# A three-layer interaction network on one core: four chunks' h1 kept, M in array quarters, V1 and V0 moved to VectorE

## The chip, the cores and the metric

The kernel runs on one core of a Trainium2 chip. The metric is the device time of one execution in microseconds, taken as the median of three timed runs. A profile of one more execution shows, for every engine, what ran when and what ended each wait.

## What is computed

The input x has 1024 samples, 64 fields and 16 embedding columns (all float32). Three layers multiply the field matrix with itself:

```python
x0 = x; h = x; xs = []
for i in range(3):
    z = einsum('bfe,bge->bfge', x0, h).reshape(B, 64 * fh, 16)
    y = einsum('oc,bce->boe', W[i], z) + b[i]
    if i != 2:
        x_i, h = y[:, :64], y[:, 64:]
    else:
        x_i, h = y, y
    xs.append(x_i)
out = sum(concatenate(xs, axis=1), axis=2) @ fc_w.T + fc_b
```

## The kernel before, in words

Everything behind the hidden halves is linear up to the final sum, so the kernel never forms layers two and three in full. With u = x1 (the hidden half of layer one, "h1") the result is a sum over products of two factors. The kernel makes h1 = W0[64:]·z, a second factor from a 64x64x64 array M (W1[64:] contracted with V2, where V2 is W2 weighted by fc_w) and V1 (W1[:64] weighted by fc_w), and a term in V0 (W0[:64] weighted by fc_w).

The 1024 samples are cut into 32 chunks of 512 columns. For each chunk c, `product(c, j)` on VectorE makes four z tiles of 128x2048 (line 159), and `contract` / `contract_last` (lines 167 and 183) multiply 16 slices of z and one last tile `zl` with `w_all`, 17 weight tiles of 128 columns: columns 0 to 63 give h1 ("part 0"), columns 64 to 127 give the second factor ("part 1"). A whole chunk is 17 matmuls, and each float32 matmul appears as two records. `factors` then multiplies the two halves, `sums` reduces them, `v0x` adds the V0 term once for each pair of chunks.

Part 1 of `w_all` is not there at the start. The setup is a chain: W2 is loaded and weighted (line 273, `pv2`), copied and written back transposed (`v2t`), M is made by 64x64 matmuls (line 296, `pm`) and copied to `m_sb` (line 297), `m_sb` is written to DRAM as `md` (lines 298 to 304), read back skewed as `ms` on the SP and ACT queues (lines 330 and 335), and added into part 1 of `w_all` (line 341). While this goes on, the first NF = 3 chunks go through `side_by_side` (line 224): 64 weight columns, two column halves of the chunk beside each other in the array, part 0 only. When part 1 is there, the same three chunks are run with part 1. Their z tiles are kept until then; the pool `zp` has 13 of them. V1 and V0 are made by eight matmuls on TensorE (line 355, `pv01`), copied by ScalarE and moved into `w_all` and `bd` by DMA.

The order of the instructions on each engine and on each queue is the order of the program text. The tile pools decide when a buffer can be written again: `xa` and `xb` have two buffers each, the `set` tiles of the setup two.

Of the kernel before, what the change touches and what calls it, by code (L numbers as in the profile page):

```python
# [45 lines left out]
NF = 3  # L46
# [3 lines left out]
def cin_kernel(ctx, tc, xra, xrb, w0p, w0d, w1h, wv2, w01, b0, b1, b2, fc_w, fc_b, out):  # L50
# [52 lines left out]
    fv2 = const_tile("fv2", [128, 32])  # L103
    fv01 = const_tile("fv01", [128, 32])
    nc.gpsimd.memset(fv01, 0.0)
    nc.gpsimd.tensor_copy(fv2, fc2.to_broadcast([128, 32]))
    for n in range(2):
        nc.gpsimd.tensor_copy(
            fv01[halves[n], 16 * n : 16 * n + 16], fc01[halves[n]].to_broadcast([F, 16])
        )  # L110
# [60 lines left out]
    def last_tile(c):  # L171

        zl = xp.tile([128, N], F32, tag="zl", name=f"zl_{c}", bufs=4)
        nc.scalar.activation(zl[0:64], xas[c][0:64, 0, :], AF.Square)  # L174
        nc.scalar.copy(zl[64:128], xas[c][64:128, 0, :])  # L175
        if c % 2 == 0:
            xxs[c // 2] = sp.tile([128, N], F32, tag="xx", name=f"xx_{c}", bufs=3)
        to = halves[c % 2]
        nc.scalar.copy(xxs[c // 2][to], xas[c][to, 0, :])  # L179
        zls[c] = zl  # L180
# [25 lines left out]
    def sums(k, rows, parts):  # L206
# [7 lines left out]

    H2 = N // 2

    def side_by_side(c, part, tiles):
        cols = slice(part * F, (part + 1) * F)  # L220
        for t in tiles:
            z = zls[c] if t == NT else zs[c, t // NI][:, t % NI, :]
            for n in range(2):
                nc.tensor.matmul(  # L224
                    accs[c][halves[n], part * H2 : (part + 1) * H2],
                    w_all[:, t, cols], z[:, n * H2 : (n + 1) * H2],
                    start=(t == 0), stop=(t == NT), skip_group_check=True,
                )

    def group(j):  # L230
        return range(j * NI, (j + 1) * NI)

    def first_factors(c):
        uu = uu_tile(c)
        q = sp.tile([128, H2], F32, tag="q", name=f"q_{c}")
        nc.scalar.copy(q, accs[c][:, H2:N])
        for n in range(2):
            at = halves[n]
            nc.vector.scalar_tensor_tensor(
                uu[:, n * H2 : (n + 1) * H2], accs[c][at, 0:H2], bh1[at], q[at],  # L240
                ALU.add, ALU.mult,
            )

    def h1_weights(tiles):
# [4 lines left out]
    for c in range(NF):
        new_acc(c)  # L250
    last_tile(0)
    product(0, 0)
    h1_weights(slice(0, NI))
    side_by_side(0, 0, group(0))
    product(0, 1)

    nc.vector.memset(w0s[64:128, 3 * NI, 1, :], 0.0)
    h1_weights(slice(NI, NT))
    nc.vector.tensor_copy(w_all[0:64, NT, 0:64], w0ds)
    side_by_side(0, 0, group(1))  # L260
    product(0, 2)
    side_by_side(0, 0, group(2))
    product(0, 3)
# [20 lines left out]
    side_by_side(0, 0, group(3))  # L284
    side_by_side(0, 0, [NT])
# [4 lines left out]
    m_sb = z_tile("m_sb").rearrange("p i n -> p (i n)")  # L290
    m_lo, m_hi = [m_sb[to].rearrange("p (f g) -> p f g", g=F) for to in halves]
    for m in range(4):
        pm = ps.tile([128, 512], F32, tag="set", name=f"pm_{m}")
        cols = slice(m * 512, (m + 1) * 512)
        for to in halves:
            nc.tensor.matmul(pm[to], v2t[to], w1s[to, cols], start=True, stop=True)  # L296
        nc.scalar.copy(m_sb[:, cols], pm)
    nc.scalar.dma_start(out=md[0:64, 0:32, :], in_=m_lo)
    nc.scalar.dma_start(out=md[0:64, 32:64, :], in_=m_hi)
    nc.sync.dma_start(out=md[0:64, 64:96, :], in_=m_lo)  # L300
    nc.sync.dma_start(out=md[64:96, 32:64, :], in_=m_hi[0:32])
    nc.scalar.dma_start(out=md[64:96, 0:32, :], in_=m_lo[0:32])
    nc.sync.dma_start(out=md[64:96, 64:68, :], in_=m_lo[0:32, 0:4, :])  # L303
    nc.sync.dma_start(out=md[64:68, 68:96, :], in_=m_lo[0:4, 4:32, :])

    last_tile(1)
    for j in range(NJ):
        product(1, j)
        side_by_side(1, 0, group(j))
    side_by_side(1, 0, [NT])  # L310
    last_tile(2)
    for j in range(NJ):
        product(2, j)
        side_by_side(2, 0, group(j))
    side_by_side(2, 0, [NT])
# [35 lines left out]
    v01r = const_tile("v01r", [128, 2, 512])  # L351
    for n in range(2):
        pv = ps.tile([128, 512], F32, tag="set", name=f"pv01_{n}")
        for k in range(4):
            nc.tensor.matmul(  # L355
                pv[32 * k : 32 * k + 32], fv01, w01s[n][:, k * 512 : (k + 1) * 512],
                start=True, stop=True,
                tile_position=(0, 32 * k),
            )
        nc.scalar.copy(v01r[:, n, :], pv)  # L360
        v0, v1 = [
            v01r[16 * v : 128 : 32, n, :].rearrange("k (f g) -> k f g", g=F) for v in range(2)
        ]
        at = slice(32 * n, 32 * n + 32)
        nc.scalar.dma_start(out=w_all[64 + 32 * n : 96 + 32 * n, NT, 64:128], in_=v1)
        for to in halves:
            nc.scalar.dma_start(out=bd[to.start + 32 * n : to.start + 32 * n + 32, to], in_=v0)
    for c in range(3, 5):
        last_tile(c)
        for j in range(NJ):  # L370
            product(c, j)
# [126 lines left out]
```

## Time and profile before

| | us |
|---|---|
| median of three runs | 535.95 (535.71 to 536.26) |
| the profiled execution | 535.2 |
| its span in the trace | 533.4 |
| TensorE busy | 500.3 |
| VectorE busy | 341.4 |
| ScalarE busy | 81.7 |

Times in the rows count from the start of the span. A chain row gives start, length and what the chain of work went through. A timeline row gives start, length, engine, line, operation and how many instructions are merged in it. The profiled execution takes 1.8 us more than its span, and the median 0.75 us more than the profiled execution.

### The profile page before, as it was taken

The numbers are of one execution on the slowest core, as the hardware profiler recorded it, in microseconds if no ns is written. First come the engines' busy times: TensorE is split into PE (matmuls) and PEld (weight loads), VectorE is DVE, ScalarE is ACT, GpSimd is POOL, SyncE is SP. The second block draws the span as 40 slices with busy tenths as digits, with TensorE's granted clock in tenths as the row PEclk, the third lists the DMA queues.
The fourth block names the chain that finished last, engine by engine and source line by source line (L and its number), as shares of the span: only waits on it lengthen the run. The fifth ranks groups of instructions, "written<-read, shape, count | busy, mean of one in ns | idle before, by whom it ended". The sixth has DMA issues, their size and how long they took to land.

```text
span 533.4 us, 3675 instructions
## 1 busy us (share of the span) xinstructions
PE 500.3 (94%) x1490; PEld 228.2 (43%) x1490; DVE 341.4 (64%) x203; ACT 81.7 (15%) x141; POOL 7.0 (1%) x23
## 2 busy tenths in 40 slices
PE   2769299999999999999999999999999999999996
PEld 1336165444444444444444444444444444444442
DVE  3592159998939487694939487593939487591103
ACT  2012005111111111011111111011111111010001
POOL 5000000000000000000000000000000000000000
PEclk9979699999999999999999999999999999999999
DMA  7937774564443405144443505144443505100000
GB/s 266 422 114 179 192 334 159 204 237 194 159 157 127 188 20 227 69 157 159 157 157 120 194 17 222 77 159 157 158 157 114 202 11 227 79 0 0 0 1 0
DMA packets 14373, 76.97 MB, mean 144 GB/s; under 512 B 4336, under 2 KB 4880, under 8 KB 5396
## 3 DMA queue, kind: packets, MB, share of 16 engines
q1 hardware_dynamic: 12072, 74.81, 37.0%
q10 hardware_dynamic: 1964, 1.92, 1.7%
q8 instruction: 12, 0.20, 0.1%
q0 software_dynamic: 320, 0.00, 0.0%
q14 instruction: 5, 0.04, 0.0%
HBM read 74.48 MB, written 2.16 MB: 144 GB/s over the span
## 4 chain that ended last, share of the span: by engine, by line
PE 90%; DMA 6%; DVE 1%; SPq 1%; ACT 0%; ACTq 0%; issue 0%; DVEq 0%
PE acc L167 75%; PE acc L224 6%; PE acc L183 5%; PE y L201 3%; DMA ms<-md 2%; DMA xb<-in_xrb 2%; DMA md<-m_sb 2%; DMA v2t<-v2r 1%; PE pm L296 1%; DVE z L159 0%; ACTq L280 0%; PE po L402 0%; SPq L303 0%; PE pv L355 0%; DVE w_all L341 0%
## 5 line engine op out<-in xcount | busy, mean ns | idle before, releaser
L167 PE MATMUL acc<-z,w_all 128*128 128x512 f32 x928 | 405.5, 592 | 0.0
L159 DVE TENSOR_TENSOR z<-xa,xb 128x2048 f32<-128x2048 f32 x128 | 284.4, 2283 | 25.4 <-DMA xb<-in_xrb 25.4
L167 PEld LDWEIGHTS acc<-z,w_all 128*128 128x128 f32 x928 | 176.2, 190 | 222.3 <-issue 216.3
L224 PE MATMUL acc<-z,w_all 128*64 128x256 f32 x384 | 48.6, 416 | 22.2 <-DVE w_all L245 11.5
L194 ACT COPY q<-acc 64x512 f32<-64x512 f32 x29 | 16.9, 582 | 341.8 <-PE acc L183 331.0
L195 DVE SCALAR_TENSOR_TENSOR uu<-acc,bh,q 64x512 f32<-64x512 f32 x29 | 21.6, 743 | 65.8 <-ACT q L194 65.4
L204 DVE SCALAR_TENSOR_TENSOR uu<-y,cx,xx 128x512 f32<-128x512 f32 x16 | 12.0, 750 | 79.0 <-PE y L201 78.9
L224 PEld LDWEIGHTS acc<-z,w_all 128*64 128x64 f32 x384 | 29.3, 150 | 41.2 <-DVE w_all L245 12.3
L183 PE MATMUL acc<-zl,w_all 128*128 128x512 f32 x58 | 29.6, 592 | 0.0
L174 ACT ACTIVATE zl<-xa 64x512 f32<-64x512 f32 x32 | 20.1, 630 | 18.2 <-DMA xa<-in_xra 9.6
L208 DVE TENSOR_REDUCE acc<-uu 128x64 f32<-128x1024 f32 (+2 forms) x18 | 20.2, 1129 | 0.6
L175 ACT COPY zl<-xa 64x512 f32<-64x512 f32 x32 | 19.7, 615 | 0.4
L179 ACT COPY xx<-xa 64x512 f32<-64x512 f32 x32 | 19.6, 613 | 0.4
L183 PEld LDWEIGHTS acc<-zl,w_all 128*128 128x128 f32 x58 | 11.0, 190 | 13.9 <-issue 13.9
L201 PE MATMUL y<-xx,bd 128*128 128x512 f32 x32 | 16.4, 595 | 0.0
L296 PE MATMUL pm<-w1s,v2t 64*64 64x512 f32 x16 | 6.0, 909 | 6.6 <-DMA v2t<-v2r 6.6
L201 PEld LDWEIGHTS y<-xx,bd 128*128 128x128 f32 x32 | 6.0, 190 | 7.6 <-issue 7.6
L340 DVE MEMSET ms<- 64x64 f32 x1 | 0.1, 112 | 12.3 <-DMA ms<-md 12.3
L360 ACT COPY v01r<-pv 128x512 f32<-128x512 f32 x2 | 1.2, 588 | 35.7 <-PE pv L355 33.8
L296 PEld LDWEIGHTS pm<-w1s,v2t 64*64 64x64 f32 x16 | 2.4, 209 | 9.8 <-DMA v2t<-v2r 7.0
L341 DVE TENSOR_TENSOR w_all<-ms 128x1024 f32<-128x1024 f32 x1 | 1.2, 1224 | 5.7 <-DMA ms<-md 5.7
L408 ACT ACTIVATE res<-po,cst 2x480 f32<-2x480 f32 (+1 forms) x2 | 0.9, 465 | 25.2 <-PE po L402 25.2
(42 smaller groups left out, 31.4 us busy)
## 6 DMA issues: line engine op xcount, KB each, us to landing
xa<-in_xra SPq DMA_DIRECT2D x32, 1024.0 KB
xb<-in_xrb SPq DMA_DIRECT2D x31, 1024.0 KB
w<-in_wv SPq DMA_DIRECT2D x2, 1024.0 KB
w<-in_w SPq DMA_DIRECT2D x2, 1024.0 KB
w1s<-in_w1h SPq DMA_DIRECT2D x1, 1024.0 KB
md<-m_sb ACTq DMA_DIRECT2D x2, 512.0 KB
xb<-in_xrb SPq DMA_DIRECT2D x1, 768.0 KB
w0s<-in_w0p SPq DMA_DIRECT2D x1, 768.0 KB
```

The source lines that it names most:

```text
L159: nc.vector.tensor_tensor(z, xas[c], xbs[c][:, j, :].unsqueeze(1).to_broadcast([128, NI, N]), ALU.mult)
L167: nc.tensor.matmul(accs[c], w_all[:, t, :], zs[c, j][:, i, :], start=(t == 0), stop=False)
L174: nc.scalar.activation(zl[0:64], xas[c][0:64, 0, :], AF.Square)
L175: nc.scalar.copy(zl[64:128], xas[c][64:128, 0, :])
L179: nc.scalar.copy(xxs[c // 2][to], xas[c][to, 0, :])
L183: nc.tensor.matmul(accs[c], w_all[:, NT, :], zls[c], start=False, stop=True)
L194: nc.scalar.copy(q, accs[c][64:128])
L195: nc.vector.scalar_tensor_tensor(uu, accs[c][0:64], bh1[0:64], q, ALU.add, ALU.mult)
L201: nc.tensor.matmul(ys[k], bd, xxs[k], start=True, stop=True)
L208: nc.vector.tensor_reduce(acc[rows, parts, k, :], uus[k][rows, parts].rearrange("p k (b e) -> p k b e", e=E), AX.X, ALU.add,)
L224: nc.tensor.matmul(accs[c][halves[n], part * H2 : (part + 1) * H2], w_all[:, t, cols], z[:, n * H2 : (n + 1) * H2], start=(t == 0), stop=( ...
L296: nc.tensor.matmul(pm[to], v2t[to], w1s[to, cols], start=True, stop=True)
```

## The change

The first NF = 4 chunks go through part 0 before M is there, and their h1 is kept in SBUF with its bias (`hb`, 256 columns in 128 partitions for each chunk), so that the PSUM bank and the z tiles can be given away. Part 1 of chunks 2 and 3 is run as soon as part 1 of the weights is there, from the z tiles still held. Chunks 0 and 1 are loaded and multiplied once more and run with part 1 behind chunk 7 (`order`). M is made in four 64x64 quarters of the array, two PSUM tiles at a time, and `md` is written in other pieces. V1 and V0 are products and sums on VectorE (`weigh`). The first loads are packed so that x and the weights of one group j come together, and chunk 1 is loaded ahead of `w1s`.

```diff
-NF = 3
+NF = 4
-    zp = ctx.enter_context(tc.tile_pool(name="zp", bufs=13))
+    zp = ctx.enter_context(tc.tile_pool(name="zp", bufs=12))
-    ps = ctx.enter_context(tc.tile_pool(name="ps", bufs=3, space=bass.MemoryType.PSUM))
+    ps = ctx.enter_context(tc.tile_pool(name="ps", bufs=2, space=bass.MemoryType.PSUM))
...
+    for at in ((0, 0, 2), (0, 2, 4), (1, 0, 4)):
+        nc.sync.dma_start(out=xw[at[0]][:, at[1] : at[2], :], in_=xw0[at[0], :, at[1] : at[2], :])
...
     for k in range(2):
-        nc.sync.dma_start(out=w2s[k], in_=wv2[:, k * 2048 : (k + 1) * 2048])
+        nc.sync.dma_start(out=w2s[k], in_=w2t[k])
+    load_chunk(1)
     nc.sync.dma_start(out=w1s, in_=w1h)
-    load_chunk(1)
...
+    def half_contract(c, part, j):
+
+        cols = slice(part * F, (part + 1) * F)
+        rows = slice(0, F) if part == 0 and j == NJ else slice(0, 128)
+        for t in (NT,) if j == NJ else range(j * NI, (j + 1) * NI):
+            z = zls[c] if t == NT else zs[c, j][:, t % NI, :]
+            for n in range(2):
+                nc.tensor.matmul(
+                    accs[c][halves[n]], w_all[rows, t, cols], z[rows, n * H2 : (n + 1) * H2],
+                    start=(t == 0), stop=(t == NT),
+                )
+
+    def keep_h1(c):
+        nc.scalar.activation(hb[:, c, :], accs[c], AF.Identity, bias=bh1)
...
+        if c < NF:
+            for n in range(2):
+                at = halves[n]
+                nc.vector.tensor_tensor(
+                    uu[:, n * H2 : (n + 1) * H2], accs[c][at], hb[at, c, :], ALU.mult
+                )
+            return
...
+    for j in range(3, NJ + 1):
+        half_contract(0, 0, j)
+    keep_h1(0)
+    squares(1)
+    new_acc(1, H2)
     for j in range(NJ):
         product(1, j)
+    for j in range(3):
+        half_contract(1, 0, j)
+    m_sb = z_tile("m_sb")
+    pms = []
+    for m in range(0, NI, 2):
+        pms += [ps.tile([128, N], F32, tag="set", name=f"pm_{m + n}") for n in range(2)]
+        for n in range(2):
+            for h in range(2):
+                e = 2 * n + m // 2
+                nc.tensor.matmul(
+                    pms[m + n][halves[h ^ n]], v2t[halves[h]],
+                    w1s[halves[h], e * N : (e + 1) * N], start=True, stop=True,
+                )
+        for n in range(2):
+            nc.scalar.copy(m_sb[:, m + n, :], pms[m + n])
+    load_chunk(3)
...
+    def quarter(rows, first):
+        return md[rows, first : first + 16, :].rearrange("r (m f) g -> r m (f g)", m=2)
+
+    for n in range(2):
+        at = 64 * n
+        f0 = 16 * n
+        nc.scalar.dma_start(out=quarter(slice(0, 64), f0), in_=m_sb[halves[n], n::2, :])
+        nc.scalar.dma_start(out=quarter(slice(0, 64), 32 + f0), in_=m_sb[halves[1 - n], n::2, :])
+        nc.sync.dma_start(out=quarter(slice(32, 64), 64 + f0), in_=m_sb[at + 32 : at + 64, n::2, :])
+        nc.sync.dma_start(out=quarter(slice(64, 96), 32 + f0), in_=m_sb[64 - at : 96 - at, n::2, :])
+        nc.sync.dma_start(out=quarter(slice(64, 68), 64 + f0), in_=m_sb[at : at + 4, n::2, :])
+    nc.sync.dma_start(
+        out=md[68:96, 64:68, :].rearrange("r f g -> r (f g)"), in_=m_sb[4:32, 0, 0:256]
+    )
+    for j in range(3, NJ + 1):
+        half_contract(1, 0, j)
+    keep_h1(1)
+    for c in range(2, NF):
+        last_tile(c)
+    for c in range(2, NF):
+        new_acc(c, H2)
+        for j in range(NJ):
+            product(c, j)
+        for j in range(NJ + 1):
+            half_contract(c, 0, j)
+    keep_h1(2)
     ms = set_tile("ms").rearrange("p (v t g) -> p v t g", v=2, g=F)
...
     nc.sync.dma_start(out=w_all[0:64, NT, 64:128], in_=skewed(0, [[1, F]]))
+    keep_h1(3)
...
-    w01s = [set_tile(f"w01_{k}") for k in range(2)]
-    for k in range(2):
-        nc.sync.dma_start(out=w01s[k], in_=w01[:, k * 2048 : (k + 1) * 2048])
-    load_chunk(3)
     load_chunk(4)
-    side_by_side(0, 1, range(NT))
-    side_by_side(1, 1, range(NT))
+    w1x = set_tile("w1x")
+    nc.sync.dma_start(out=w1x, in_=wx1)
+    for c in range(2, NF):
+        new_acc(c, H2)
+        for j in range(NJ):
+            half_contract(c, 1, j)
+
+    def weigh(w, fc, out):
+        nk, n = out.shape[-1], fc.shape[-1]
+        w = w.rearrange("p (k c) -> p k c", c=n)
+        nc.vector.tensor_tensor(w, w, fc.unsqueeze(1).to_broadcast([128, nk, n]), ALU.mult)
+        nc.vector.tensor_reduce(out, w, AX.X, ALU.add)
+
+    last_tile(4)
+    for j in range(NJ):
+        product(4, j)
+    v1h = const_tile("v1h", [128, 32])
+    weigh(w1x, fcr[:, 64:128], v1h)
     for n in range(2):
-        pv = ps.tile([128, 512], F32, tag="set", name=f"pv01_{n}")
...
+        nc.vector.tensor_copy(
+            w_all[64:128, NT, 64 + 32 * n : 96 + 32 * n], v1h[halves[n]]
+        )
+    load_chunk(5)
+    w0x = set_tile("w0x")
+    nc.sync.dma_start(out=w0x, in_=wx0)
...
+    for c in range(2, NF):
+        half_contract(c, 1, NJ)
+    last_tile(5)
+    for j in range(NJ):
+        product(5, j)
+    v0h = const_tile("v0h", [128, 32])
+    weigh(w0x, fcr[:, 0:64], v0h)
+    for to in halves:
+        for n in range(2):
+            nc.vector.tensor_copy(bd[to, to.start + 32 * n : to.start + 32 * n + 32], v0h[halves[n]])
+    for c in range(2, NF):
+        factors(c)
...
+    order = [4, 5, 6, 7, 0, 1] + list(range(8, NCH))
+    for s, c in enumerate(order):
...
+        if s + 2 < len(order):
+            ahead = order[s + 2]
+            load_chunk(ahead)
+            last_tile(ahead)
             for j in range(NJ):
+                product(ahead, j)
```

## Rows read from the trace of the kernel before

**Rows 1.** The page: span, and busy time of each engine.
```profile
span 533.4 us, 3675 instructions
PE 500.3 (94%) x1490; PEld 228.2 (43%) x1490; DVE 341.4 (64%) x203; ACT 81.7 (15%) x141; POOL 7.0 (1%) x23
```

**Rows 2.** The chain in order of time, 0 to 130 us.
```profile
25.47 6.13 DMA v2t<-v2r
31.61 6.03 PE pm L296 x16
37.66 0.59 ACT m_sb L297
41.34 8.93 DMA md<-m_sb
51.70 4.56 DMA ms<-md
56.28 5.17 DMA ms<-md
61.84 1.24 DVE w_all L341
63.12 15.96 PE acc L224 x128
79.07 1.85 PE pv L355 x16
81.31 8.35 PE acc L224 x76
90.72 6.87 PE acc L167 x16
```

**Rows 3.** The end of that chain, 500 to 534 us.
```profile
527.79 0.87 PE acc L183 x2
528.66 0.02 issue
```

**Rows 4.** Windows of 10 us: busy and count by engine, granted clock, DMA share, GB/s.
```profile
50.00:60.00 10.00, 2.45 (x24) 1.34 (x20) 0.11 (x1) 0.00 (x0) 0.00 (x0) 0.84 0.79 191
60.00:70.00 10.00, 6.88 (x46) 4.18 (x48) 1.22 (x1) 0.00 (x0) 0.00 (x0) 0.65 0.64 243
```

**Rows 5.** The timeline, 0 to 50 us.
```profile
26.08 17.70 DVE L159 TENSOR_TENSOR z<-xa,xb 128x2048 f32<-128x2048 f32 x8 [6.46 <-DMA xb<-in_xrb]
37.55 7.13 PE L224 MATMUL acc<-z,w_all 128*64 128x256 f32 x64
38.27 0.48 SPq L300 DMA_DIRECT2D md<-m_sb  x1
44.94 5.35 PE L224 MATMUL acc<-z,w_all 128*64 128x256 f32 x48
```

**Rows 6.** Windows of 1 us, same columns as rows 4.
```profile
22.00:23.00 1.00, 1.00 (x12) 0.29 (x6) 0.00 (x0) 0.50 (x1) 0.00 (x0) 1.00 1.03 426
42.00:43.00 1.00, 1.00 (x13) 0.64 (x11) 1.00 (x1) 0.33 (x1) 0.00 (x0) 1.00 1.03 213
```

**Rows 7.** The costliest groups of the page.
```profile
L159 DVE TENSOR_TENSOR z<-xa,xb 128x2048 f32<-128x2048 f32 x128 | 284.4, 2283 | 25.4 <-DMA xb<-in_xrb 25.4
L208 DVE TENSOR_REDUCE acc<-uu 128x64 f32<-128x1024 f32 (+2 forms) x18 | 20.2, 1129 | 0.6
L296 PE MATMUL pm<-w1s,v2t 64*64 64x512 f32 x16 | 6.0, 909 | 6.6 <-DMA v2t<-v2r 6.6
L174 ACT ACTIVATE zl<-xa 64x512 f32<-64x512 f32 x32 | 20.1, 630 | 18.2 <-DMA xa<-in_xra 9.6
```

**Rows 8.** The SP and ACT queues' timeline, 49 to 62 us.
```profile
51.08 5.78 ACTq L335 DMA_DIRECT2D ms<-md  x4
...
56.00 0.59 SPq L346 DMA_DIRECT2D w<-in_w  x1
```

**Rows 9.** DMA queues, 58 to 59 us, then 60 to 61 us: packets, MB, share (q1 is SP's, q10 ACT's).
```profile
q1 hardware_dynamic: 42, 0.34, 89.1%
...
q1 hardware_dynamic: 33, 0.14, 33.7%
q10 hardware_dynamic: 272, 0.07, 29.7%
```

More of the change, by code (lines that the diff above doesn't have):

```diff
@@ L45, with cin_kernel @@
 EXT = 96
-NF = 3
+NF = 4
 @with_exitstack
-def cin_kernel(ctx, tc, xra, xrb, w0p, w0d, w1h, wv2, w01, b0, b1, b2, fc_w, fc_b, out):
+def cin_kernel(ctx, tc, xra, xrb, xw0, w0d, w1h, w2t, wx1, wx0, b0, b1, b2, fc_w, fc_b, out):
     nc = tc.nc
@@ L73, in cin_kernel @@
     fc2 = const_tile("fc2", [128, 1])
-    fc01 = const_tile("fc01", [128, 1])
     bh1 = const_tile("bh1", [128, 1])
@@ L81, in cin_kernel @@
     nc.gpsimd.dma_start(out=fc2, in_=fc_w[0, 128:256].unsqueeze(1))
-    nc.gpsimd.dma_start(out=fc01, in_=fc_w[0, 0:128].unsqueeze(1))
+    nc.gpsimd.dma_start(out=w0ds, in_=w0d)
     for to in halves:
@@ L89, in cin_kernel @@
     for n in range(2):
+        nc.gpsimd.dma_start(
+            out=fcol[:, n : n + 1], in_=fc_w[0, n * 128 : (n + 1) * 128].unsqueeze(1)
+        )
         nc.gpsimd.dma_start(out=fcb[n : n + 1], in_=fc_b.unsqueeze(1))
+    nc.gpsimd.dma_start(
+        out=fcr, in_=bass.AP(tensor=fc_w.tensor, offset=0, ap=[[0, 128], [1, 128]])
+    )
+    fv2 = const_tile("fv2", [128, 32])
+    nc.gpsimd.tensor_copy(fv2, fc2.to_broadcast([128, 32]))
     ones = const_tile("ones", [128, 2])
@@ L101, in cin_kernel, with load_xa @@
     nc.gpsimd.memset(bd, 0.0)
[L103 to L110, printed above, removed]
     xas, xbs, zls, xxs = {}, {}, {}, {}
-    def x_tiles(c):
+    def load_xa(c):
         xas[c] = xp.tile([128, NI, N], F32, tag="xa", name=f"xa_{c}")
-        xbs[c] = xp.tile([128, NJ, N], F32, tag="xb", name=f"xb_{c}")
-    def load_xa(c):
         nc.sync.dma_start(
@@ L159, in product, with squares, last_tile @@
         nc.vector.tensor_tensor(
-            z, xas[c], xbs[c][:, j, :].unsqueeze(1).to_broadcast([128, NI, N]), ALU.mult
+            z, xas[c], xbs[c][j].unsqueeze(1).to_broadcast([128, NI, N]), ALU.mult
         )
         zs[c, j] = z
+    def squares(c):
+        zls[c] = xp.tile([128, N], F32, tag="zl", name=f"zl_{c}", bufs=4)
+        nc.scalar.activation(zls[c][0:64], xas[c][0:64, 0, :], AF.Square)
+    def last_tile(c):
+        squares(c)
+        nc.scalar.copy(zls[c][64:128], xas[c][64:128, 0, :])
+        if c % 2 == 0:
+            xxs[c // 2] = sp.tile([128, N], F32, tag="xx", name=f"xx_{c}", bufs=3)
+        to = halves[c % 2]
+        nc.scalar.copy(xxs[c // 2][to], xas[c][to, 0, :])
     def contract(c, j):
@@ L169, in contract @@
             )
[L171 to L180, printed above, removed]
     def contract_last(c):
         nc.tensor.matmul(accs[c], w_all[:, NT, :], zls[c], start=False, stop=True)
+    H2 = N // 2
+    def half_contract(c, part, j):
[10 more added lines that the diff above has]
+        nc.scalar.activation(hb[:, c, :], accs[c], AF.Identity, bias=bh1)
     def uu_tile(c):
@@ L204, in x_v0x, with sums @@
         nc.vector.scalar_tensor_tensor(uus[k][:, 1, :], ys[k], cx, xxs[k], ALU.add, ALU.mult)
-    def sums(k, rows, parts):
+    def sums(k, rows=slice(0, 128), parts=slice(0, 2)):
         nc.vector.tensor_reduce(
@@ L213, in sums, with h1_weights @@
         )
[L217 to L244, printed above, removed]
+    def h1_weights(j):
         nc.vector.tensor_tensor(
-            w_all[:, tiles, 0:64], w0s[:, tiles, 0, :], w0s[:, tiles, 1, :], ALU.add
+            w_all[:, j * NI : (j + 1) * NI, 0:64], w0s[j][:, :, 0, :], w0s[j][:, :, 1, :], ALU.add
         )
[L249 to L258, printed above, removed]
+    new_acc(0, H2)
+    squares(0)
+    for j in range(NJ):
+        product(0, j)
+        if j == NJ - 1:
+            nc.vector.memset(w0s[j][64:128, 0, 1, :], 0.0)
+        h1_weights(j)
     nc.vector.tensor_copy(w_all[0:64, NT, 0:64], w0ds)
[L260 to L263, printed above, removed]
+    for j in range(3):
+        half_contract(0, 0, j)
     load_chunk(2)
@@ L283, in cin_kernel @@
             )
-    side_by_side(0, 0, group(3))
-    side_by_side(0, 0, [NT])
-    md = dr.tile([EXT, EXT, F], F32, tag="md", name="md")
[L290 to L306, printed above, removed]
+    for j in range(3, NJ + 1):
+        half_contract(0, 0, j)
@@ L307, in cin_kernel @@
+    keep_h1(0)
+    squares(1)
+    new_acc(1, H2)
     for j in range(NJ):
         product(1, j)
[L309 to L315, printed above, removed]
+    for j in range(3):
+        half_contract(1, 0, j)
[12 more added lines that the diff above has]
+            nc.scalar.copy(m_sb[:, m + n, :], pms[m + n])
@@ L339, in cin_kernel @@
     nc.sync.dma_start(out=w_all[0:64, NT, 64:128], in_=skewed(0, [[1, F]]))
+    keep_h1(3)
     nc.vector.memset(ms[64:128, 1, 3 * NI, :], 0.0)
     nc.vector.tensor_tensor(w_all[:, 0:NT, 64:128], ms[:, 0], ms[:, 1], ALU.add)
-    w01s = [set_tile(f"w01_{k}") for k in range(2)]
-    for k in range(2):
-        nc.sync.dma_start(out=w01s[k], in_=w01[:, k * 2048 : (k + 1) * 2048])
-    load_chunk(3)
     load_chunk(4)
-    side_by_side(0, 1, range(NT))
-    side_by_side(1, 1, range(NT))
-    v01r = const_tile("v01r", [128, 2, 512])
-    for n in range(2):
-        pv = ps.tile([128, 512], F32, tag="set", name=f"pv01_{n}")
[L354 to L371, printed above, removed]
+    w1x = set_tile("w1x")
[14 more added lines that the diff above has]
+    weigh(w1x, fcr[:, 64:128], v1h)
+    for n in range(2):
+        nc.vector.tensor_copy(
+            w_all[64:128, NT, 64 + 32 * n : 96 + 32 * n], v1h[halves[n]]
+        )
+    load_chunk(5)
+    w0x = set_tile("w0x")
+    nc.sync.dma_start(out=w0x, in_=wx0)
     cx = const_tile("cx", [128, 1])
@@ L409, in finish @@
         nc.scalar.dma_start(out=outs[:, pairs, :], in_=res[:, pairs, :])
-    everyone, first, last = slice(0, NP), slice(0, NP - 1), slice(NP - 1, NP)
-    for c in range(NF, NCH + 1):
+    order = [4, 5, 6, 7, 0, 1] + list(range(8, NCH))
+    first, last = slice(0, NP - 1), slice(NP - 1, NP)
+    for s, c in enumerate(order):
         k = c // 2
-        if c + 2 < NCH:
-            load_chunk(c + 2)
-            last_tile(c + 2)
+        if s + 2 < len(order):
+            ahead = order[s + 2]
+            load_chunk(ahead)
+            last_tile(ahead)
@@ L417, in cin_kernel @@
             for j in range(NJ):
-                product(c + 2, j)
-        if c < NCH:
-            new_acc(c)
-            contract(c, 0)
-            contract(c, 1)
-            if c % 2:
-                v0x(k)
-            if c == NCH - 1:
-                pool(first, 1)
-                pool(first, 0)
-            contract(c, 2)
-            contract(c, 3)
+                product(ahead, j)
+        new_acc(c, H2 if c < NF else N)
+        for j in range(NJ):
+            if j == 2:
+                if s == 1:
+                    v0x(NF // 2 - 1)
+                if c % 2:
+                    v0x(k)
+                if s == len(order) - 1:
+                    pool(first, 1)
+                    pool(first, 0)
+            if c < NF:
+                half_contract(c, 1, j)
+            else:
+                contract(c, j)
@@ L430, in cin_kernel @@
+        if c < NF:
+            half_contract(c, 1, NJ)
+        else:
             contract_last(c)
-        if c == NCH - 1:
+        if s == len(order) - 1:
             finish(first)
-        if c - 1 < NF:
-            first_factors(c - 1)
-        else:
-            factors(c - 1)
+        if s:
+            factors(order[s - 1])
+        if s == 1:
+            x_v0x(NF // 2 - 1)
+            sums(NF // 2 - 1)
         if c % 2:
             x_v0x(k)
-            if c == NCH - 1:
-                sums(k, slice(0, 128), slice(1, 2))
-                sums(k, slice(0, 64), slice(0, 1))
-                pool(last, 1)
-        elif c < NCH:
-            sums(k - 1, slice(0, 128), slice(0, 2))
-        else:
-            sums(k - 1, slice(64, 128), slice(0, 1))
-            pool(last, 0)
-            finish(last)
+        elif s:
+            sums(order[s - 1] // 2)
@@ L451 @@
+    sums(NP - 1, parts=slice(1, 2))
+    sums(NP - 1, slice(0, 64), slice(0, 1))
+    pool(last, 1)
+    factors(NCH - 1)
+    sums(NP - 1, slice(64, 128), slice(0, 1))
+    pool(last, 0)
+    finish(last)
 def kernel(r_x, L0_rec_W0, L0_rec_b0, L0_rec_W1, L0_rec_b1, L0_rec_W2, L0_rec_b2, L0_rec_fc_w, L0_rec_fc_b):
```

61 lines of the change are left out of this document (31 added, 30 removed).

## The prediction

> **What bounds the kernel now.** First the page's busy times: TensorE works 500.3 of 533.4 us, VectorE 341.4, ScalarE 81.7 [rows 1]. So what counts is TensorE's list of work and the holes in it. The chain in order of time says where the holes are. From 63.12 us, when part 1 of the weights is there, the chain is TensorE alone until the last contraction ends at 528.66 [rows 2, 3]: 465.5 us without a hole that matters. Before 63.12 it is the setup: v2t lands at 31.6, M's matmuls take 6.03 us and the last copy ends at 38.25, `md` is written until 50.27, `ms` read until 61.45, then the add [rows 2]. TensorE meanwhile does three chunks' part 0 and stands still from about 52.5 on: the window from 50 to 60 has 2.45 us of it busy [rows 4]. So there are two ways to a shorter time: less TensorE work behind the point where the weights are ready (I call it M), and an earlier M. The reader should see that work moved ahead of M is free as long as TensorE waits there.
>
> Yardsticks: a whole chunk is 34 records at 6.87/16 = 0.429 us, 14.6 us [rows 2]. Half a chunk, 68 records of 256 columns, took 44.94 - 37.55 = 7.39 us [rows 5]. The sum is made against the profiled execution (535.2 us, 1.8 above its span); the median is 0.75 above that, and I carry differences over to it. About 0.2% (1.1 us) is what a measurement of this kernel can tell from no change.
>
> **Work behind M.** Before: 3 half chunks, 29 whole ones, V1 and V0's matmuls. After: 4 halves, 28 wholes, no such matmuls. The difference is +7.4 - 14.6 - 1.85 (line 355) = -9.1 us [rows 2, 5]. The sixteen V0 terms, the two small constants and the whole tail stay as they are.
>
> **What covers it.** The fourth chunk's part 0 must fit before M. VectorE sets its end: chunk 1 now lands one 1 MB load earlier (`w1s` goes behind it), 1.05 MB at 426 GB/s is 2.5 us [rows 6], so at 26.1 - 2.5 = 23.6 [rows 5]; twelve products at 2.283 us [rows 7] end at 51.0, and the last group and last tile at about 53. That is well before M near 61, so the cover is about 8 us; were it gone, the 7.4 us would be paid.
>
> **VectorE behind M.** V1 costs it one 128x2048 multiplication (2.28), a sum over 2048 elements per partition (twice the 1.13 of line 208, 2.3; the mean mixes forms, up to 2.5) and two copies of 32 columns (between nothing and the 0.63 of a 512-column operation on ScalarE; I take 0.1 each) [rows 7]. With chunk 4's four products, 9.1, V1 is there 14 to 15 us after chunk 4 can start. TensorE's last tiles of chunks 2 and 3 want it 15.96 us after M, the length of the same 128 records before [rows 2]. So there is 1 to 2 us of slack, if chunk 4 has landed by then. Its two loads stand in SP's queue where line 346 stood; that 1 MB was still moving in the window from 60 to 61, so the second MB comes 2.5 later, at about M + 0.5 [rows 8, 9]. V0 follows with another 9.1 + 4.7 us, done at about M + 28, and is wanted in the middle of chunk 5, at about M + 16.5 + 0.9 + 14.6 + 7 = M + 39. Four half-size products with `hb` take the place of three half-size q copies and six sums. Making chunks 0 and 1 again adds 8 x 2.28 = 18.3 us to VectorE and 4 MB of loads. VectorE then has about 341 + 18 + 9 = 368 of some 520 us. The two halves of chunks 0 and 1 take TensorE only 14.8 us, VectorE's two products 18.3; but z tiles for two chunks are made ahead, so this is paid from the lead and made up at 4 to 5 us a chunk afterwards. Price: nothing.
>
> **M itself.** M's matmuls now stand behind three groups of chunk 1. The third z is ready at 23.6 + 3 x 2.28 = 30.4, its 16 records take 1.8 us, or about twice that at the lower clock: TensorE comes to M at 32.2 to 33.6, I take 33.0. v2t landed at 31.6 before [rows 2] and its matmuls have not moved back, so it does not set this. Before, from the first matmul to the last copy was 6.64 us. The 16 records are 16 x 0.909 = 14.5 us long and ran in 6.03 [rows 7, 2], so at least two quarters ran at a time. With four the floor is four copies of 0.59 plus a first pair of about 0.8, 3.2 us; the ceiling is 6.64. I take 3.5, as two tiles are filled for each wait: `m_sb` at 36.5, 1.75 earlier.
>
> Here a rule weighs against: the Trainium skill, "TensorEngine Tiling (Array Packing)", "Gotcha 1: PSUM Pressure", says that different row tiles cannot access one PSUM bank at the same time, and both row halves write one `pm` tile. The 14.5 us of records in 6.03 do not look like it; by that rule M would stay at 6.6 us and cost 1.8 us of the sum, since chunk 3's load hides the rest.
>
> `md`: the code writes 1.63 MB where it wrote 2.16 (the sizes of the transfers added up). At the 213 GB/s of the window from 42 to 43 [rows 6] that is 7.7 us for 10.1. But chunk 3's 2.1 MB now go ahead of it in SP's queue: its xa waits for the last product of chunk 1 (32.7), its bytes flow from about 33.7 to 38.6. From 37.5 the `md` bytes share the engines, so all is through at 33.7 + 4.9 + 7.7 = 46.3, landed at 47.3, for 50.27 before: 3.0 earlier. The eleven writes (seven before) are queued on SP and ACT; behind ACT's stand six copies of about 0.62 [rows 7] and `keep_h1(2)`, which waits for chunk 2's last group (products end at 41.9, group and tile 2.2, so 44.5 with the copy) and holds back ACT's half of `ms`: a floor of about 45.
>
> `ms`: 50.27 to 63.1 before, 12.8 us. What can change it is the bulk behind it. ACT's four small reads were issued over 5.78 us, SP's next load at 56.00 [rows 8]; from 58 to 59 only SP's queue moved bytes, and from 60 to 61, when its 1 MB ran out, ACT's 272 packets came [rows 9]. So bulk that is issued first goes first. Now chunk 4, `w1x` and chunk 5 (5 MB) stand there. At least today's 1 MB goes ahead; each further MB costs 2.5 us. Two to three may be issued before ACT's last read; I take +1.2, between none and one more.
>
> The skill's "DMA: Bandwidth & Descriptors", "Queues, rings and completion order", says that each engine goes round-robin between the queues, a packet at a time. By that rule the bulk adds nothing to `ms`, and the time would be 523.8. The rows from 58 to 61 agree with it only if the whole 1 MB was one packet on each engine.
>
> M: 47.3 + 12.8 + 1.2 = 61.3, for 63.1: 1.8 earlier. The clock after it: it had fallen before M (the mean 0.84 over 50 to 60 is 3.2 us at the lower level, 1.2 GHz, so from 56.8, after 4.4 us of standing still) and stayed there until 67 (0.65 over 60 to 70) [rows 4]. About 8 us of standing still remain, so I take the same loss; without it 15.96 would be 2 x 7.13, 1.7 us less [rows 2, 5].
>
> **Sum.** 9.1 + 1.8 = 10.9 us: 535.95 - 10.9 = 525.0.
>
> **Rivals.**
> 1. *M not earlier, or later.* Four quarters bring nothing, chunk 3 ahead of `md` and two more MB ahead of ACT's reads: `md` lands at 50.5, M = 50.5 + 12.8 + 5 = 68.3, 5.2 later: 532. With one of these, 527.5 to 531. For it: SP's and ACT's queues are fuller at each of these places. Against: the engines stood idle between chunk 2 and `md` before.
> 2. *`md` much faster.* If its bytes flow at the 426 GB/s of the loads, 3.8 us, ACT's floor of 45 holds: M at 57.8, 5.3 earlier: 521.5. For it: the writes now come from both halves of the partitions; against: 213 GB/s at a full DMA share.
> 3. *V1 comes too late.* If chunk 4 lands 5 us behind M, TensorE waits 3 to 4 us at the last tiles: 528.5. Against: the queue's order.
> 4. *Slower: writes cost by the piece.* `md` was written in 8 KB rows, some 260 pieces; now 784 pieces of 2 KB. If each took an engine the 10.1 x 16 / 260 = 0.62 us of an 8 KB piece, 784 would take 30 us, M would come 22 us later, and the time would be 547. It turns slower from M 9 later on, that is at about 0.38 us a piece; proportional to bytes would be 0.16. Against: `ms` reads of 256 bytes moved 2048 packets in some 10 us.
>
> **Chances.** The forecast, 523 to 527.5: 0.55. Rival 1 (527.5 to 531): 0.20. Rival 2: 0.13. Rival 3: 0.06. Rival 4: 0.04. Within 0.2%: 0.02. Faster 0.94, same 0.02, slower 0.04. For 8 in 10: from rival 2's end, 521, to 530.5, in rival 1; no wider, as the 9.1 us are counted from rows.
>
> **What would show it.** After: no matmul for V1 or V0, 28 whole chunks; the part 1 add ending near 61 and TensorE unbroken from there over some 456.4 us; `keep_h1(3)` near 53, before `ms` lands; `m_sb` near 36.5, `md` landing near 47. Wrong if TensorE waits behind M, at the last tiles of chunks 2 and 3, in chunk 5 for V0 or around chunks 0 and 1; or if `md` or `ms` takes longer than before.

## The result, and the profile after

The changed kernel took 523.4 us (521.13 to 524.37) where the kernel before took 536.11 in the same comparison: a ratio of 0.9758, 95% interval 0.9725 to 0.9790. The forecast was 525.0, in a range of 521.0 to 530.5. The profiled execution took 523.09 us, 12.1 less than the one before. Executions that took twice the usual time or more (one of e9's, 1084.63 us, and e1's profiled one, 2096.04 us) are left out of all medians and ratios below. That the number was met says little by itself: two rivals came true together, with opposite signs.

The page of the kernel after: span, and busy time of each engine.
```profile
span 521.3 us, 3859 instructions
PE 496.5 (95%) x1576; PEld 228.0 (44%) x1576; DVE 370.6 (71%) x224; ACT 81.8 (16%) x141; POOL 9.4 (2%) x23
```
TensorE lost 3.8 us of work and VectorE gained 29; TensorE is still the bound [rows 1].

The chain of the kernel after in order of time, 0 to 130 us, then its end.
```profile
23.29 6.71 DVE z L157 x3
31.99 1.06 PE pm L298 x8
34.83 1.09 ACT m_sb L303 x2
36.17 6.48 DMA md<-m_sb
43.13 2.38 DMA md<-m_sb
46.41 5.09 DMA ms<-md
52.67 6.59 DMA xb<-in_xrb
59.34 3.75 DVE z L157 x2
68.24 2.21 DVE w1x L379
70.48 2.30 DVE v1h L380
73.22 1.97 PE acc L196 x8
75.19 15.47 PE acc L178 x32
...
515.64 0.87 PE acc L183 x2
```
Beside [rows 2, 3] two things are to be seen. From M's matmuls on, which start at 31.9 for 31.6 before, each step of the setup is shorter. And the chain does not pass from the add to TensorE as it did before: it goes through chunk 4's load, its products and V1 on VectorE, and joins TensorE at 73.22, at the last tiles of chunks 2 and 3.

| us from the start of the span | before | after | forecast |
|---|---|---|---|
| last copy to `m_sb` ends | 38.25 | 35.92 | 36.5 |
| `md` landed | 50.27 | 45.51 | 47.3 |
| the add of part 1 ends (M) | 63.1 | 54.8 | 61.3 |
| last contraction ends | 528.66 | 516.51 | 517.8 |
| from M to there | 465.5 | 461.6 | 456.4 |

So M came 8.3 us earlier, not 1.8, and the stretch behind it shrank by 3.9, not 9.1. The timeline of the kernel after, 45 to 62 us, shows the queues around M.
```profile
46.41 5.11 ACTq L357 DMA_DIRECT2D ms<-md  x4
...
52.11 0.52 SPq L120 DMA_DIRECT2D xa<-in_xra  x1
...
53.05 0.47 ACT L202 ACTIVATE hb<-acc,bh 128x256 f32<-128x256 f32 x1 [7.16 <-DMA ms<-md]
53.60 1.22 DVE L364 TENSOR_TENSOR w_all<-ms 128x1024 f32<-128x1024 f32 x1 [1.93 <-DMA ms<-md]
54.88 7.34 PE L196 MATMUL acc<-z,w_all 128*64 128x256 f32 x66 [1.88 <-DVE w_all L364]
59.34 4.49 DVE L157 TENSOR_TENSOR z<-xa,xb 128x2048 f32<-128x2048 f32 x2 [4.51 <-DMA xb<-in_xrb]
```
ACT's last read of `ms` was out at 51.52, 0.6 us ahead of SP's next large load; before, the load had gone first [rows 8]. The fourth h1 is kept from 53.05 on, as forecast. But M is now so early that chunk 4, at 59.3, lands 4.5 us behind it.

What TensorE waited for around M, from its waits between 30 and 130 us, and the windows of the wait for V1 (columns as in rows 4).
```profile
PE acc L196 <- DVE w_all L389: 3.9, 1, 3.9
PE acc L196 <- DVE w_all L364: 1.9, 1, 1.9
```
```profile
71.00:72.00 1.00, 0.00 (x0) 0.00 (x0) 1.00 (x1) 0.25 (x1) 0.00 (x0) 0.71 1.03 410
73.00:74.00 1.00, 0.78 (x4) 0.53 (x6) 0.97 (x2) 0.00 (x0) 0.00 (x0) 0.50 1.02 426
77.00:78.00 1.00, 1.00 (x3) 0.48 (x2) 1.00 (x2) 0.04 (x1) 0.00 (x0) 0.50 0.06 16
78.00:79.00 1.00, 1.00 (x4) 0.46 (x3) 1.00 (x1) 0.00 (x0) 0.00 (x0) 0.87 0.00 0
```
TensorE stands still for 3.9 us, from 69.3 on, until line 389 has put V1 in place. Meanwhile the clock falls to its lower level, 1.2 GHz: the mean of 0.71 in the window from 71 to 72 puts the fall at about 71.4, and the 0.87 from 78 to 79 the rise at about 78.3.

### The profile page after: what moved, and what is told of

Its sections match the earlier page's. It is cut to its first block, busy times and chain, and to the rows that moved or that the text cites. A ratio compares the mean times of both kernels' runs of the same rounds, so it can differ in the third digit from the quotient of the medians.

```text
span 521.3 us, 3859 instructions
## 1 busy us (share of the span) xinstructions
PE 496.5 (95%) x1576; PEld 228.0 (44%) x1576; DVE 370.6 (71%) x224; ACT 81.8 (16%) x141; POOL 9.4 (2%) x23
## 4 chain that ended last, share of the span: by engine, by line
PE 86%; DMA 8%; DVE 4%; SPq 1%; ACT 0%; issue 0%; ACTq 0%; DVEq 0%
PE acc L178 74%; DMA xb<-in_xrb 5%; PE acc L183 5%; PE acc L196 4%; DVE z L157 3%; PE y L225 3%; DMA md<-m_sb 2%; DMA ms<-md 1%; DVE v1h L380 0%; DVE w1x L379 0%; PE pm L298 0%; PE po L432 0%; ACT m_sb L303 0%; SPq L120 0%; SPq L136 0%
## 5 line engine op out<-in xcount | busy, mean ns | idle before, releaser
L178 PE MATMUL acc<-z,w_all 128*128 128x512 f32 x896 | 393.2, 594 | 0.0
L157 DVE TENSOR_TENSOR z<-xa,xb 128x2048 f32<-128x2048 f32 x132 | 295.8, 2286 | 39.1 <-PE acc L178 30.9
L178 PEld LDWEIGHTS acc<-z,w_all 128*128 128x128 f32 x896 | 170.6, 191 | 215.7 <-issue 210.2
L196 PE MATMUL acc<-z,w_all 128*64 128x256 f32 x512 | 60.4, 393 | 15.8 <-DVE w_all L240 11.7
L196 PEld LDWEIGHTS acc<-z,w_all 128*64 128x64 f32 x512 | 36.8, 141 | 39.9 <-DVE w_all L240 11.7
L157 DVE TENSOR_TENSOR z<-xa,xw 128x2048 f32<-128x2048 f32 x4 | 9.1, 2284 | 9.0 <-DMA xw<-in_xw 9.0
L196 PE MATMUL acc<-zl,w_all 64*64 64x256 f32 (+1 forms) x32 | 5.8, 457 | 3.9 <-DVE w_all L389 3.9
L196 PEld LDWEIGHTS acc<-zl,w_all 64*64 64x64 f32 (+1 forms) x32 | 2.1, 154 | 6.2 <-DVE w_all L389 4.0
L432 PE MATMUL po<-acc,ones 128*2 128x480 f32 (+1 forms) x8 | 2.3, 386 | 2.0 <-DVE acc L232 2.0
L202 ACT ACTIVATE hb<-acc,bh 128x256 f32<-128x256 f32 x4 | 1.9, 474 | 14.0 <-DMA ms<-md 7.2
```

The lines of the kernel that those rows point to most:

```text
L157: nc.vector.tensor_tensor(z, xas[c], xbs[c][j].unsqueeze(1).to_broadcast([128, NI, N]), ALU.mult)
L178: nc.tensor.matmul(accs[c], w_all[:, t, :], zs[c, j][:, i, :], start=(t == 0), stop=False)
L196: nc.tensor.matmul(accs[c][halves[n]], w_all[rows, t, cols], z[rows, n * H2 : (n + 1) * H2], start=(t == 0), stop=(t == NT),)
```

## The experiments

Theory A: the change gives 9.1 us of list behind M and an early M, and loses part of it at the wait for V1. Theory B, in several forms: what is taken away comes back elsewhere. The label of each run is in its heading; below, a run is called by the first part of its label.

**Last tiles behind chunk 4 (e1_last_tiles_late).**
```diff
-    for c in range(2, NF):
-        half_contract(c, 1, NJ)
...
         if s == 0:
+            for b in range(2, NF):
+                half_contract(b, 1, NJ)
+            for b in range(2, NF):
+                factors(b)
...
```
The load and the products of the chunk after next go behind them.

> The changed kernel with one move: the last tiles of chunks 2 and 3 (part 1), which wait for V1, stand behind chunk 4 on TensorE, and their factors behind that on VectorE. Theory A (the change lost part of its gain at that wait: 3.9 us of standing still, and about 2.6 us because the clock then ran at its lower level from 71.7 to 78.1): both come back, TensorE goes from the add without a break, 523.4 - 6.5 = 517. Theory B (the wait only moves on, to chunk 4's products, to V0 in chunk 5 or to chunks 0 and 1, since VectorE is the shortage there): 522 to 524, with a new wait of about the same length in the trace.

Three executions took 516.67 to 518.42 us (median 518.32), a ratio of 0.9682 (0.9658 to 0.9707) to before. 5.1 of the 6.5 us come back. That is theory A by times alone, as there is no trace of such an execution.

**V1 first (e2_v1_first).** The load of `w1x` and `weigh` go ahead of chunk 4's.
```diff
-    load_chunk(4)
     w1x = set_tile("w1x")
     nc.sync.dma_start(out=w1x, in_=wx1)
+    load_chunk(4)
...
-    last_tile(4)
-    for j in range(NJ):
-        product(4, j)
     v1h = const_tile("v1h", [128, 32])
     weigh(w1x, fcr[:, 64:128], v1h)
...
+    last_tile(4)
+    for j in range(NJ):
+        product(4, j)
```


> The changed kernel with V1's data loaded ahead of chunk 4's, and V1 made ahead of chunk 4's products on VectorE. Theory A (the wait for V1 is all that is lost behind the add): V1 there at about 61, chunk 4's first product at about 64, before TensorE wants it at 70: no wait, about 517. Theory B (chunk 4's products are then late instead): TensorE waits at chunk 4 for 2 us or more, and the time stays at 521 to 524.

517.48 us (516.75 to 518.89), ratio 0.9680 (0.9657 to 0.9703). The chain of this run, 0 to 115 us, from the add on.
```profile
54.17 1.24 DVE w_all L364
55.45 15.72 PE acc L196 x128
71.55 1.01 PE acc L196 x8
72.56 13.93 PE acc L178 x32
86.49 0.86 PE acc L183 x2
```
Now the chain is TensorE without a break. Against the kernel after, the eight records take 1.01 for 1.97 us and the 32 take 13.93 for 15.47: the wait cost 3.9 us of standing and 2.5 of clock. Chunk 4 is no new bound. This settles the wait for V1. The two spans differ by less than that 6.4, by 4.2: in this execution, the slowest of the four, the clock fell at M instead, the 128 records took 15.72 for 14.03 us, and M is 0.6 later.

**Chunk 4 ahead of the ms reads (e3_chunk4_ahead_of_ms).** `load_chunk(4)` moves ahead of the loop that reads `ms`.

> The changed kernel with chunk 4's 2 MB put ahead of the ms reads in SP's queue. Theory A (bytes that are issued first go first, on all queues): ms lands up to 4.9 us later, the add ends at about 59 instead of 54.8; chunk 4 is there, so no wait for V1; the clock is lost once, before the add instead of at V1; in sum about as before, 522 to 525. Theory B (the engines take turns between the queues): ACT's half of ms is not delayed, SP's half is; the add ends within 2 to 3 us of 54.8, and the time is 518 to 521.

522.79 us (521.72 to 524.7). The add ends at 58.4. ACT's reads of `ms` were issued from 45.67 to 49.45; its queue's bytes are seen in the DMA queues of the windows from 49 to 50 and from 52 to 53 us (q1 is SP's, q10 ACT's).
```profile
q1 hardware_dynamic: 47, 0.39, 100.9%
...
q10 hardware_dynamic: 743, 0.21, 100.0%
q1 hardware_dynamic: 84, 0.07, 23.0%
```
Until 50 only the bulk of SP's queue moved, although ACT's reads had been out for up to four microseconds; in the kernel after, where no bulk stood ahead of them, the first bytes of ACT's queue came 2.3 us after the issue. Bytes that were issued first went first, across the two queues: theory A, in the time too. But ACT's half is not what ended last here. SP's own small reads were held until 53.4, and the add waited last for `w_all<-md`, which stands behind them in SP's queue and landed at 57.17:
```profile
DVE w_all L365 <- DMA w_all<-md: 2.9, 1, 2.9
```
The turn for each queue that the Trainium skill describes ("DMA: Bandwidth & Descriptors", "Queues, rings and completion order") is not seen here at a scale that would help a small read. That the rule fails is not shown either: the prediction's condition for it, 1 MB as one packet on each engine, was not tested.

**The kernel before, bulk behind ACT's reads (e11_before_bulk_behind, e12_before_bulk_on_act).** The first try exchanged the two `w01` loads, the second moved them and the loads of chunks 3 and 4 to ACT's queue. The diff is that of the second.
```diff
-        nc.sync.dma_start(out=w01s[k], in_=w01[:, k * 2048 : (k + 1) * 2048])
+        nc.scalar.dma_start(out=w01s[k], in_=w01[:, k * 2048 : (k + 1) * 2048])
...
-        nc.sync.dma_start(
+        (nc.scalar if c in (3, 4) else nc.sync).dma_start(
```


> The kernel before, with the two w01 loads exchanged: the first now waits for the buffer of ms, so that no bulk load is issued before ms has landed. Theory A (bytes that were issued first go first; the 1 MB of w01 went ahead of ACT's last read of ms): ms lands 2 to 2.5 us earlier, the add ends at about 60.5 instead of 63.1, the time is 533 to 534. Theory B (the last read is late for its own sake): 535 to 537.

> The kernel before, with the loads that follow the ms reads (w01 and chunks 3 and 4) moved from SP's queue to ACT's, where they stand behind ACT's own ms reads; all else as before. The run with the exchanged w01 loads did not keep the bulk behind: 1 MB was again issued ahead of the add. Theory A (1 MB ahead of ACT's last read of ms costs its 2.5 us): ms lands at about 59, the add ends near 60.6 instead of 63.1, the time is 2 to 2.5 us less than before, 533. Theory B (the last read is late for its own sake, and bulk takes turns with it): no change within 1 us.

e11: 534.78 us, ratio 0.9998 (0.9985 to 1.0011), and it tests nothing: the load that now came first was issued at 56.66 all the same, and ACT's last read took 5.20 us, as before. e12: 531.84 us (530.63 to 532.97), ratio 0.992 (0.9902 to 0.9938), 4.3 us, more than the 2 to 2.5 expected. Its chain, 28 to 75 us:
```profile
51.94 4.75 DMA ms<-md
56.72 2.30 DMA ms<-md
59.29 1.24 DVE w_all L341
```
ACT's last read landed 2.30 us after its issue, for 5.17 before [rows 2]: theory A. From `md` landed (51.2) to the add's end is 9.4 us, for 12.8 before; in the changed kernel it is 9.3. So of M's 8.3 us, some 3.5 can be had without the rest of the change: they are which of two queues issued first. (The other parts are 2.3 us up to `m_sb` and 2.4 for `md`.) That the whole run gained 4.3 us is more than this explains: its profiled execution gained 2.2.

**Why md is faster (e4_before_md_halves_swapped, e5_before_md_2kb_pieces, e8_md_one_half_first, e9_before_md_alternating).** In e4 ACT's first two writes are exchanged; in e5 each large write is cut in two with pieces of 2 KB; e9 also alternates the halves; e8 takes the alternation out of the kernel of e2.
```diff
-    nc.scalar.dma_start(out=md[0:64, 0:32, :], in_=m_lo)
...
+    def pieces(queue, rows, first, src):
+        for n in range(2):
+            queue.dma_start(
+                out=md[rows, first : first + 32, :].rearrange("r (m n f) g -> r m n (f g)", m=2, n=2)[:, :, n, :],
+                in_=src.rearrange("r (m n f) g -> r m n (f g)", m=2, n=2)[:, :, n, :],
+            )
+    pieces(nc.scalar, slice(0, 64), 0, m_lo)
```


> The kernel before, with ACT's first two writes of md exchanged: ACT begins with the upper 64 partitions while SP begins with the lower 64. Theory A (md was slow, 213 GB/s, because both queues read the same 64 partitions at a time): the writes go at 350 GB/s or more together, md lands about 4 us earlier than at 50.3, and the time is 532. Theory B (the size of the pieces, 8 KB, or writing itself sets the rate): md lands within 1 us of 50.3 and the time stays at 536.

> The kernel before, with each of the five large writes of md cut in two interleaved ones, so that its pieces are 2 KB with gaps between them and no longer 8 KB; the bytes stay 2.16 MB. Theory A (8 KB pieces are written at half of the rate of 2 KB pieces: an engine took about 0.6 us for 8 KB before, 0.08 us for 2 KB after): the bytes pass in 5 to 6 us instead of 10, md lands at 46 to 47 instead of 50.3, the time is 531 to 533. Theory B (the rate changed for another reason, such as fewer bytes or the order of the queues): md lands at 50 or later because of the five more transfers, 536 to 537.

> The kernel of the run with V1 first; the eleven writes of md are the same, but each queue has those that read the lower 64 partitions first and then those of the upper 64. Theory A (64 partitions give half of the rate, and md is fast after the change because its writes alternate between the halves and overlap): the md bytes go at 200 to 250 GB/s once chunk 3 is through, md lands 2 to 3 us later than in that run (46.3), the add ends 2 to 3 us later, the time is 519.5 to 521. Theory B (it is fast for another reason, such as short transfers): md lands within 0.7 us of it, 517 to 518.5.

> The kernel before, with md written by ten interleaved writes as in the run with 2 KB pieces, but alternating between the lower and the upper 64 partitions on each queue, the two queues in opposite phase. Theory A (halves that alternate overlap): 300 to 400 GB/s, md lands at 46 to 47, the time is 531 to 532. Theory B (something else than the halves): 200 to 240 GB/s as in that run, md lands at 50, 533 to 536.

e4: 535.62 us, ratio 1.0009 (0.9998 to 1.002); `md` landed at 49.85, 0.4 us earlier, and `ms` was issued at 49.94. e5: 533.95 us, ratio 0.9976 (0.9955 to 0.9997); `md` landed at 50.24. Its windows from 40 to 49 move 199 to 281 GB/s with pieces of 2 KB, two of them (columns as in rows 4):
```profile
41.00:42.00 1.00, 1.00 (x13) 0.64 (x11) 1.00 (x2) 0.00 (x0) 0.00 (x0) 1.00 0.97 201
42.00:43.00 1.00, 1.00 (x12) 0.71 (x10) 1.00 (x1) 0.00 (x0) 0.00 (x0) 1.00 0.99 203
```
What its profiled execution gained lies in `ms`, by the same race as e12: the issue of SP's load began first, at 56.22, but was through only at 57.8, behind that of ACT's last read (57.2), which landed in 2.42 us. e8: 518.53 us (516.82 to 519.24), the writes take 10.3 us from first issue to landing as in e2. e9: 534.46 us, ratio 0.9986 (0.9974 to 0.9997), 11.4 us, for 12.0 before; two of its windows reach 289 and 322 GB/s, but not the mean. Neither the size of the pieces nor the half of the partitions that is read explains it; the theories on `md` that were tried fell. Not tried: that in the changed kernel the writes pile up behind chunk 3's load and then flow together.

**One h1 behind the add (e6_one_h1_behind, e10_h1_behind_reordered).** In e10 chunk 3's part 0 stands behind chunk 2's part 1.
```diff
         for j in range(NJ):
             half_contract(c, 1, j)
+        if c == 2:
+            for j in range(NJ + 1):
+                half_contract(3, 0, j)
+            keep_h1(3)
```


> The kernel of the run with V1 first, with one edit: TensorE makes chunk 3's part 0 behind the add of part 1 instead of ahead of it; its products stay where they were. Theory A (TensorE's list behind the add sets the time, and part 0 ahead of it is free): 7.4 us more, 517.5 + 7.4 = 525, less nothing. Theory B (the h1 kept ahead only fills a list that VectorE or the loads set): 517.5 to 520.

> The kernel of the run with V1 first; chunk 3's part 0 now stands behind chunk 2's part 1 on TensorE, so that it cannot run ahead of the add (the edit before left TensorE's order as it was). Theory A (the list behind the add sets the time): 7.4 us more, 517.5 + 7.4 = 524.9, or 0.5 us less if the clock falls alike. Theory B (the list is set by VectorE or loads): 517 to 520.

e6's edit moved nothing on TensorE, since chunk 3's part 0 only passed lines of other engines; its 518.49 us (518.05 to 519.08) is a second sample of e2's kernel, and shows that 1 us between such medians means little. e10 took 526.3 us (526.03 to 526.75). Its timeline, 50 to 85 us:
```profile
54.63 16.41 PE L196 MATMUL acc<-z,w_all 128*64 128x256 f32 x128 [8.81 <-DVE w_all L364]
70.97 0.65 PE L196 MATMUL acc<-zl,w_all 64*64 64x256 f32 x4
71.56 7.13 PE L196 MATMUL acc<-z,w_all 128*64 128x256 f32 x64
```
TensorE now stands still for 8.8 us ahead of the add and pays 64 + 4 records behind it. The spans differ by 524.6 - 517.1 = 7.5 us and the medians by 8.8, for the 7.4 of half a chunk: theory A. Work ahead of M is free here, behind it it costs its full length.

**M one group earlier (e7_m_one_group_earlier).** From e2: M's matmuls behind two groups of chunk 1 instead of three, `keep_h1(2)` behind ACT's `ms` reads.

> The kernel of the run with V1 first, with M's matmuls one group of chunk 1 earlier on TensorE, and the copy of chunk 2's h1 behind ACT's reads of ms. Theory A (M is set by the products of chunk 1 and by that copy, as predicted): m_sb 2 us earlier, the add at about 53.5 instead of 55.4, when TensorE has just finished chunk 3's part 0: 515 to 516, and the clock no longer falls ahead of the add. Theory B (v2t or chunk 3's load ahead of md sets it): the add within 0.5 us of 55.4, 517 to 518.

517.11 us (516.9 to 517.5), ratio 0.9668 (0.9642 to 0.9694), the best version run, but not to be told from e2. `m_sb` is 1.2 us earlier (35.1), `md` lands at 45.6 for 46.1 and the add ends at 55.2 for 55.4. SP's second group of `md` writes was issued at 41.68 for 39.69 in e2: the queue that also holds chunk 3's load ate the gain. This fits theory B, in the form that names that load; the load was not moved to show it.

## Why the prediction was right, and where it was not

- *The work behind M, -9.1.* Right: e10 gives half a chunk back at 7.5 in spans, and e2's chain is unbroken. The cover too: h1 of chunk 3 was kept at 53.5 against a forecast of 53. It was thinner than thought, as M moved: TensorE stands still for 1.9 us ahead of the add, not 8.
- *M's matmuls and copies.* Forecast 33.0 to 36.5, 3.5 us; measured 31.99 to 35.92, 3.9 us. The number was about right, the reason given for it was not. The prediction reads the 6.6 us of before as two quarters at a time and gives the gain to four. It overlooks the clock, in windows of the kernel before (columns as in rows 4), and what it did to the time from one copy to the next:
```profile
34.00:35.00 1.00, 1.00 (x4) 0.35 (x2) 1.00 (x2) 0.28 (x1) 0.00 (x0) 0.50 0.00 0
37.00:38.00 1.00, 1.00 (x8) 0.34 (x6) 1.00 (x2) 0.73 (x2) 0.00 (x0) 1.00 0.00 0
```
```profile
33.69 0.59 ACT L297 COPY m_sb<-pm 128x512 f32<-128x512 f32 x1 [8.82 <-PE pm L296]
35.40 0.59 ACT L297 COPY m_sb<-pm 128x512 f32<-128x512 f32 x1 [1.12 <-PE pm L296]
36.80 0.59 ACT L297 COPY m_sb<-pm 128x512 f32<-128x512 f32 x1 [0.82 <-PE pm L296]
37.66 0.59 ACT L297 COPY m_sb<-pm 128x512 f32<-128x512 f32 x1 [0.27 <-PE pm L296]
```
  A `pm` tile took 1.71 us at the lower level (33.69 to 35.40) and 0.86 at the higher (36.80 to 37.66). Estimated from these, four tiles and the last copy take 4 x 0.86 + 0.6 = 4.0 us at the higher level with no new quarter. Before, TensorE had stood still for 6.6 us until v2t landed [rows 7]; now M's matmuls follow three groups of chunk 1, at a granted clock of 1.00. So by this estimate nearly all of the 2.7 us is the clock; the two were not tried apart. The four quarters do run at once: the first eight records took 1.06 us (the chain, 31.99), where two quarters at a time need 2 x 0.86 = 1.7. But the copies now stand in pairs behind the matmuls, in the same chain, and take it back:
```profile
33.07 0.59 ACT m_sb L303
33.71 1.10 PE pm L298 x4
```
  The rule of the Trainium skill on row tiles and one PSUM bank that the prediction quotes ("TensorEngine Tiling (Array Packing)", "Gotcha 1: PSUM Pressure") did not show: two `pm` tiles are filled at a time, so with it the eight records would have needed the 1.7 us. The overlap of the records, which the prediction goes by, counts no quarters: whole-array records of 0.594 us in the mean start every 0.429 us as well (line 178 of the kernel after).
- *`md`.* Landed 1.8 us earlier than forecast. The step that failed is its rate, 213 GB/s: from 39 to 45 the kernel after moved 294 in the mean, the end of chunk 3's load with it, and up to 395 in one window. Why stays open.
- *`ms`, 12.8 + 1.2.* This step failed most. "Bulk that is issued first goes first" held (e3, e12), but I took the order of issue from the trace of before and added a further MB. ACT's last read went first this time, and `ms` took 9.3 us. The profiled executions agree on it: in the changed kernel, e2, e6, e7, e8 and e10 this read was out 0.5 to 1.9 us ahead of SP's next large load; in the kernel before, e4, e9 and e11 the load was out first. What turned the order is not shown. The term should have been a choice between two outcomes 3.5 us apart, 9.3 and 12.8.
- *V1 in time.* This was rival 3, and it came. The working was right as far as it went, 13.9 us from chunk 4's start to V1 there (59.3 to 73.2, forecast 14 to 15), but its condition was written against a late M. With M at 54.8 and chunk 4 at 59.3, 4.5 us behind it for the 0.5 forecast, the 1 to 2 us of slack became a wait of 3.9. The price left out the clock: another 2.5 us (e2).
- *The clock at M.* Forecast as lost; in the profiled execution it was not, after 1.9 us of standing still: the 128 records took 14.0 us for the 15.96 of [rows 2], 2 us less. That was luck: in e6 the same 1.9 us lost it.
- *VectorE, V0, chunks 0 and 1 again.* Right: from 73.22 to 516.51 the chain of the kernel after is TensorE alone.

The sum of what I mis-sized: M 6.5 us better (54.8 for 61.3), the stretch behind it 5.2 worse (461.6 for 456.4: +3.9 wait, +2.5 clock there, -2.0 clock at M, and 0.8 that I did not follow). 1.3 us are left: that is why the number was met, and it was luck that the two nearly cancelled. Rival 2's end, an early M, and rival 3 were not independent: the earlier M is, the later V1's data are against it. I had priced them as separate cases.

## What to carry to other kernels

When a gate moves earlier, list again everything that was on time only because the gate was late, and price the gate and its next shortage as one case. Work ahead of a gate is free up to the point where the engine stops waiting for it; here the last 1.9 us of cover is what remains. Before giving a shorter stretch of matmuls to a new layout, compare the granted clock in both. A small transfer on one queue can lie behind a large one on another: what counts is whose issue is through first, and where two issues are 0.3 us apart, the forecast is two-valued.

## What the runs showed of the hardware that was not expected

- With 1 MB issued 0.3 us ahead on the other queue, a 64 KB read took 5.17 us from issue to landing (5.10 in e4, 5.20 in e11); with the bulk behind it 2.30 (e12). With 2 MB ahead (e3), ACT's reads moved no byte for over four microseconds, for 2.3 in the kernel after.
- `md` was written at 196 to 217 GB/s in the mean in the kernel before, e4, e5 and e9 (windows of 10 and 11 us around the writes), with single windows of up to 337 (e4). In the changed kernel, with the same 2 KB pieces as e5, it was 294 from 39 to 45, the end of a load included, and up to 395 in one window.
- TensorE stood still ahead of the add for 1.9 us in e6 and 2.0 in e2, and the granted clock fell at its restart in e6 and 1.0 us behind it in e2 (mean 0.83 over 50 to 60 us). After 1.9 us in the changed kernel and 2.3 in e8 it stayed up (1.00). It decides about 1.7 us (15.7 for 14.0 over the 128 records). The mean granted clock of an execution goes with its time: in e8 516.82 us at 1.000 and 518.41 to 519.24 at 0.993, in the changed kernel 521.13 at 0.993 and 523.09 to 524.37 at 0.988 to 0.991. This fits the clock as part of the spread of the new kernels; what else differs between executions was not traced.
